# Cross-attention block on one core: scores of two heads in two neighbouring PSUM banks, one ScalarE eviction for both, with order and places laid out anew

## The chip, the cores and the metric

The kernel runs on one core of a Trainium2 chip. The metric is the device time of one execution in microseconds (us). The engines are TensorE (PE, with its weight loads PEld), VectorE (DVE), ScalarE (ACT), GpSimd (POOL) and SyncE (SP), which issues the DMA transfers. Each engine takes its instructions strictly in order.

## The reference

All data are fp32. x and the context are 8 batches of 256 tokens by 512. There are 16 heads of 32, and the inner width of the last part is 2048.

```python
h = layer_norm(x, ln1_w, ln1_b)
q, k, v = (h @ q_w + q_b, ctx @ k_w + k_b, ctx @ v_w + v_b)   # 16 heads of 32
scores = where(mask, q @ k.T / sqrt(32), lowest)
out = softmax(scores) @ v
hidden = out @ cproj_w + cproj_b + x
y = gelu(layer_norm(hidden, ln2_w, ln2_b) @ fc_w + fc_b)      # 512 -> 2048
result = hidden + y @ proj_w + proj_b                          # 2048 -> 512
```

## The kernel before, in words

The tokens are worked in two halves, g = 0 and 1, of four batches (1024 tokens). The projections of q, k, v and the output `o` are done as 2 x 2 blocks with seven products instead of eight (P1 to P7, `quad`, L848); their sums of operands run on DVE and POOL (`sums`, names ending in t1 to t4, s1 to s4), and their results are added up from three PSUM banks X, Y and W (names such as k0_0_c11). The fc and proj layers use the same scheme on two levels (`grown2`), with weight sums that are stored to DRAM (fcd, prd) and loaded again (fl, pl).

Attention works in 32 units: g, a group hg of four heads, and a batch b; the names carry the three digits, so unit 020 is half 0, heads 8 to 11, batch 0. `scores` (L1009) lets PE compute, for each of the four heads j and each half kc of the keys, a block of 128 keys by 256 queries (operation s020). The four heads use 32 rows of PE each and run side by side; each head has a PSUM bank of its own. ACT then evicts each of the eight blocks (ev020_30 is head 3, key half 0) and adds a bias for each key, the mask, from `cols`. The result lies in two buffers pr of two heads each. DVE takes the maximum over the keys (mx, mt, fold; ACT moves three small pieces, mc), SP stores the maxima (md) and loads them as a broadcast to all partitions (mm). POOL or DVE subtracts them (less), ACT takes the exponential of two heads at a time (exp), and `attend` (L1057) lets PE compute the sums and the products with v in 32-column tiles (av). DVE inverts the sums (r) and scales (att). So there is a long chain between s and av of a unit, and PE works on other things meanwhile.

PE's instructions are of three kinds: full 128 x 128 matmuls, the 32-row tiles of s and the 32-column tiles of av. A transposition (turn, `turned`, L710) is a full matmul of 128 columns into a PSUM bank, four to a bank; its eviction (y0_10, L775) applies the layer norm's weight and bias. The second layer norm of half 0 has eight such groups, turn_y0_00 to turn_y0_31, and the first fc products are fc001_P1 and fc011_P1.

The order is written out: `PROGRAM` is a list of all operations by name, with a letter where an engine has to be chosen (V, A, G for DVE, ACT, POOL). `Order.run` (L94) goes through it and emits each operation's instructions on its engine. `PLACES` (L355) gives each buffer its slot in SBUF or PSUM; a later user of a slot waits for the earlier one. PSUM has eight banks of 512 columns. Three (tags W0 to W2) hold X, Y and W of the products, five (C0 to C4) the scores, av and the transpositions, unless `PLACES` names a tag of the other set.

Of the kernel before, what the change touches and what calls it, by code (L numbers as in the profile page):

```python
# [10 lines left out]
F32 = mybir.dt.float32  # L11
# [5 lines left out]
P = 128  # L17
# [6 lines left out]
BANKS = {"W": 3, "C": 5}  # L24
# [19 lines left out]
class Order:  # L44
# [49 lines left out]
    def run(self):  # L94
# [30 lines left out]
cq0_00_1 cq0_00_0 vw00 cq0_01_1 cq0_01_0 rows8 rows7 cq0_10_0 turn_c0_00 rows0 turn_c0_10 c0_00:A cq0_10_1 c0_10:V  # L125
cq0_11_0 small v0_0_P1 cq0_11_1 kw01 turn_c0_11 fw0_01_0 v0_1_P1 c0_11:A vw11 rows5 turn_c0_01 rows2 turn_c0_30
vw10 c0_01:A turn_c0_20 mk c0_30:A c0t1:G c0_20:V v0_0_t1:A vw01 turn_c0_21 v0_1_t1:V turn_c0_31 fw0_11_1 k0_0_P2
c0_21:V rows3 c0_31:V c0t2:V kw10 k0_1_P2 rows4 kw11 c0t3:V kw00 rows6 v0_0_P2 vws1:V fw0_10_0 c0t4:V fw0_00_0
v0_1_P2 vws2:V fw0_00_1 kws1:V xt0_3 rows1 k0_1_P1 fw0_10_1 kws2:V mk~1 xt0_0 kws3:V fw0_11_0 v0_0_c11 fw0i1_1:G
v0_1_P6 fw1_00_1 vws4:V xt0_2 fw0i1_2:V fw0s3:V fw1_00_0 k0_0_P1 v0_1_t2:A xt0_6 fw0i7_1:V fw1_10_0 v0_1_c11  # L130
fw0i7_2:G fw1_11_0 cols v0_1_P5 cols~1 qw10 k0_0_t1:V qw11 fw0i7_4:V fw0s1:V xt0_1 v0_0_P6 v0_1_t3:A fw1_11_1
fw0s2:V fw1_10_1 xt0_5 k0_0_P6 fw0i6_3:V xt0_4 k0_1_t1:V fw0i6_1:G cb fw0i5_1:G v0_1_P3 k0_0_t2:V kws4:G fw0i1_4:V
k0_1_P6 stats_x0_30 fw0i1_3:G fw1i1_1:V stats_x0_00 fw0i6_2:G k0_0_P5 fw1i1_3:V k0_1_t2:A xt0_7 v0_0_t2:V fw1i1_2:G
fw0_01_1 stats_x0_10 fw1i1_4:G fcd0_1_True aggr_x0_30 k0_1_P5 fw1i4_1:V qw01 aggr_x0_00 stats_x0_01 fw1i4_2:G
fw1_01_0 fw0i6_4:V fcd0_6_False stats_x0_11 k0_1_P7 k0_1_t3:A fw1_01_1 aggr_x0_01 fw0i7_3:V k0_0_t3:A eps_x0_0
fcd0_7_False stats_x0_31 pow_x0_0 qw00 aggr_x0_31 k0_1_P3 fw1i4_4:G k0_1_c22 fcd0_7_True fw0i5_2:G aggr_x0_11
# [12 lines left out]
fw0i4_3:G fcd1_5_True mc000_3 mc000_2 s020 cb1_13 mc000_1 fw1i6_3:G fold000 cb1_00 fw1i7_1:V q0_0_P3 md000 ev020_30
fw0i4_1:V ev020_21 fw1i7_2:V cb1_23 ev020_00 fw0i4_2:G cb1_21 ev020_10 fw1i7_4:G ev020_20 cb1_01 q0_1_P7 ev020_01  # L150
cb1_11 fw1i3_1:G ev020_31 q0_0_c12:A mx020_1 fw1i6_2:G ev020_11 s002 fw1i3_2:G mm000 mx020_0 fw0i4_4:G v0_1_P7
fw1i7_3:G mt020 stats_x1_11 mc020_2 mc020_3 fw1i6_4:G q0_1_t3:V ev002_30 ev002_11 fw1i3_4:G aggr_x1_10 aggr_x1_11
v0_0_P7 mc020_1 q0_1_c22 ev002_01 ev002_00 fold020 ev002_10 eps_x1_1 md020 ev002_31 pow_x1_1 ev002_20 q0_1_P3
fcd1_7_True v0_0_c22 ev002_21 cb1_31 nb_x1_1 mx002_0 less000_1:G mm020 s022 mx002_1 cb1_33 cb1_22 v0_0_P4 ev022_20
cT1_10 cb1_32 ev022_30 cT1_00 ev022_11 cb1_30 less000_0:G ev022_31 mt002 v0_1_c22 ev022_21 q0_1_P4 ev022_00 mx022_1
mc002_2 ev022_01 ev022_10 less020_0:G mx022_0 v0_1_P4 mt022 q0_1_c21 mc022_2 mc022_3 s010 mc022_1 v0_0_c21 mc002_3
exp000_0 less020_1:G cT1_01 k1_0_P1 fold022 mc002_1 ev010_20 q0_1_c12:V md022 exp000_1 v0_1_c21 fcd1_6_True cT1_20
fcd1_3_True k1_1_P1 ev010_10 ev010_31 fold002 ev010_11 cT1_11 md002 cT1_30 av000 vd0_0_11 k1_0_t1:A cT1_21 mm022
c1t1:G ev010_21 kd0_0_12 ev010_01 cT1_31 ev010_30 kd0_1_12 exp020_0 k1_0_P2 r000 mm002 ev010_00 exp020_1 att000
c1t2:V s030 norm_x1_11:A c1t3:V av020 xd1_3 ev030_10 norm_x1_10:A fcd0_4_True less022_1:G mx010_1 ev030_11 xd1_2  # L160
k1_1_t1:A k1_0_P6 xt1_7 mx010_0 ev030_21 ku003 ev030_01 ev030_20 kd0_0_22 k1_0_c11 ev030_30 ev030_31 k1_1_P6 mt010
# [12 lines left out]
mx001_0 s021 xd1_1 v1_1_t1:A ku031 norm_x1_00:A mt001 k1_1_c21 ku011 av030 ev021_00 xd1_0 norm_x1_21:V v1_0_t1:A
less032_1:G ev021_10 norm_x1_20:A v1_1_P6 mc001_3 less032_0:V xd1_4 ev021_31 ev021_20 xd1_5 mc001_2 mc001_1
vd0_1_11 ev021_30 v1_0_P6 fold001 ev021_11 ev021_21 md001 less012_0:G ev021_01 mx021_1 ku023 exp032_0 ku013 v1_0_P2
r030 exp032_1 xb1_21 xb1_20 v1_1_t2:A att030 s003 less012_1:V v1_0_t2:A mm001 av032 xb1_01 mx021_0 ev003_20
ev003_11 xb1_22 ev003_21 xb1_23 ev003_10 mt021 ev003_00 v1_0_P5 ev003_31 r032 exp012_0 att032 ev003_30 mc021_1
v1_1_P5 mx003_1 mc021_2 ev003_01 less001_0:G mc021_3 exp012_1 fold021 s023 v1_0_c11 md021 v1_1_t3:A mx003_0 xb1_13
av012 xb1_10 ev023_00 less001_1:G ev023_01 mt003 v1_0_t3:V ev023_31 ev023_21 mc003_2 v1_0_P7 mc003_3 r012 ev023_20  # L180
ev023_30 mc003_1 ev023_10 att012 ev023_11 xT1_20 s011 exp001_0 fold003 mx023_0 md003 v1_1_P2 ev011_00 mm021
ev011_31 xb1_12 ev011_11 ev011_20 xb1_11 exp001_1 v1_1_P3 xb1_03 v1_1_c11 ev011_30 mx023_1 ev011_01 ev011_21
# [329 lines left out]
def tile_xattn_block(  # L512
# [41 lines left out]
    halves = {}  # L554

    def tile_of(b):
        if b.t is None:
# [941 lines left out]
```

## Time and profile before

| | us |
|---|---|
| three runs: median (lowest, highest) | 662.69 (662.54, 663.8) |
| span of the profiled execution | 662.0 |
| PE busy in it | 654.6 |
| DVE busy | 585.7 |
| ACT busy | 342.4 |
| POOL busy | 374.8 |

Times in the profile are microseconds from the span's start unless marked ns. A group of instructions reads: line, engine, operation, what it writes and reads, partitions x elements, count; then busy time in total, mean ns of one, and the idle time of the engine ahead of them with what ended it. A row of a timeline starts with start and duration of a run of like instructions; idle time ahead of it, with what ended it, stands in brackets. The ends of matmuls are modelled, so a busy PE isn't PE at its peak. A wait is put down to the semaphore that came last.

### The profile page before, as it was taken

To read this page: it belongs to the slowest core of one execution; us is meant where nothing else is said; L and a number is where in the kernel's file an instruction comes from. 1 tells how busy PE (TensorE), PEld (TensorE's weight loads), DVE (VectorE), ACT (ScalarE), POOL (GpSimd) and SP (SyncE) were. 2 spreads that over 40 slices of the span, in tenths; PEclk is the share of its full clock that TensorE was granted. 3 is DMA by queue.
4 is the path that set the end of the run, shared out by engine and by line. 5 is a ranking of instruction groups with operands and counts; after the bars stand their busy time and mean duration, and the time that the engine had idled before them with its cause. 6 is when DMAs were issued, how large, how long until landed. Compare 5 with 4: busy or idle time off the path is not lost.

```text
span 662.0 us, 11469 instructions
## 1 busy us (share of the span) xinstructions
PE 654.6 (99%) x3925; PEld 490.0 (74%) x3925; DVE 585.7 (88%) x980; ACT 342.4 (52%) x702; POOL 374.8 (57%) x340
## 2 busy tenths in 40 slices
PE   8999999999999999999999999999999999999997
PEld 7746554477544776777688888888888888888887
DVE  2998799999999999999999998997789787998775
ACT  2046479799999899866995572030020013930000
POOL 1262773646888997699958774423535217720260
PEclk9999999999999999999999999999999999999999
DMA  8999888786574467886878698889978779359366
GB/s 250 311 356 307 211 197 291 267 255 125 144 241 161 144 202 234 263 268 197 266 249 273 198 235 225 289 269 230 195 193 241 190 201 242 93 142 240 106 141 111
DMA packets 206586, 144.84 MB, mean 219 GB/s; under 512 B 117008, under 2 KB 166976, under 8 KB 206528
## 3 DMA queue, kind: packets, MB, share of 16 engines
q1 hardware_dynamic: 206528, 144.11, 76.8%
q8 instruction: 31, 0.51, 0.3%
q14 instruction: 27, 0.22, 0.1%
HBM read 104.10 MB, written 39.98 MB: 218 GB/s over the span
## 4 chain that ended last, share of the span: by engine, by line
PE 92%; DVE 5%; ACT 1%; DMA 1%; issue 0%; SPq 0%; POOL 0%; DVEq 0%; ACTq 0%
PE pd_X L639 15%; PE fc_X L639 14%; PE fc_W L639 8%; PE av L639 7%; PE pd_W L639 7%; PE s L639 4%; PE o_X L639 4%; PE q_X L639 4%; PE k_X L639 4%; PE v_X L639 4%; PE pd_Y L639 4%; PE fc_Y L639 4%; PE q_W L639 2%; PE k_W L639 2%; PE v_W L639 2%; PE o_W L639 2%
## 5 line engine op out<-in xcount | busy, mean ns | idle before, releaser
L1047 POOL TENSOR_TENSOR pr<-pr,mm 128x512 f32<-128x512 f32 x84 | 110.4, 1346 | 22.8 <-DMA mm<-md 9.2
L619 ACT ACTIVATE pr<-s,cols 128x256 f32<-128x256 f32 x256 | 104.5, 482 | 21.8 <-PE s L639 15.8
L1022 DVE TRANSPOSE_TENSOR_REDUCE mx<-pr 128x32 f32<-128x1024 f32 x64 | 77.6, 1223 | 3.3 <-ACT pr L619 3.3
L1227 ACT ACTIVATE h<-h,cols 128x256 f32<-128x256 f32 x128 | 54.1, 498 | 36.7 <-DVE h L630 36.6
L1050 ACT ACTIVATE pr<-pr 128x1024 f32<-128x1024 f32 x64 | 66.9, 1069 | 3.4 <-POOL pr L1047 2.8
L630 DVE TENSOR_TENSOR h<-fc_X,h 128x512 f32<-128x512 f32 x80 | 52.8, 679 | 6.2 <-PE fc_X L639 5.5
L630 DVE TENSOR_TENSOR h<-fc_W,h 128x512 f32<-128x512 f32 x48 | 32.0, 679 | 5.8 <-PE fc_W L639 5.3
L639 PE MATMUL av<-pr,ones 128*32 128x256 f32 x512 | 34.2, 384 | 0.7 <-ACT pr L1050 0.6
L1029 ACT COPY mx<-mx 32x64 f32<-32x64 f32 x96 | 23.1, 243 | 19.8 <-DVE mx L1026 15.8
L1042 DVE TENSOR_TENSOR pr<-pr,mm 128x1024 f32<-128x1024 f32 x22 | 30.8, 1407 | 0.0
L628 POOL TENSOR_TENSOR z1i<-h,z1i 128x512 f32<-128x512 f32 x4 | 5.7, 1440 | 40.4 <-PE pd_X L639 40.4
L639 PEld LDWEIGHTS av<-pr,ones 128*32 128x32 f32 x512 | 14.1, 109 | 18.5 <-issue 6.7
L630 POOL TENSOR_TENSOR h<-h,fl 128x512 f32<-128x512 f32 x9 | 11.5, 1295 | 24.6 <-DVE fl L630 15.0
L639 PE MATMUL fc_W<-y1i,fl 128*128 128x256 f32 x100 | 24.6, 380 | 0.0
L639 PE MATMUL fc_X<-y1i,fl 128*128 128x256 f32 x88 | 21.6, 381 | 0.0
L639 PEld LDWEIGHTS fc_W<-y1i,fl 128*128 128x128 f32 x100 | 18.9, 190 | 2.9 <-DVE h L630 0.3
L639 PE MATMUL pd_W<-z0i,pl 128*128 128x256 f32 x88 | 20.6, 379 | 0.0
L1030 DVE TENSOR_REDUCE mx<-mx 32x32 f32<-32x256 f32 x32 | 18.4, 574 | 1.4 <-ACT mx L1029 1.3
L639 PE MATMUL pd_X<-z0i,pl 128*128 128x256 f32 x80 | 18.9, 379 | 0.0
L606 ACT COPY fl<-fc_X 128x512 f32<-128x512 f32 x6 | 3.5, 580 | 29.5 <-PE fc_X L639 29.2
L639 PEld LDWEIGHTS fc_X<-y1i,fl 128*128 128x128 f32 x88 | 16.6, 190 | 2.6 <-ACT h L606 0.2
L639 PEld LDWEIGHTS pd_W<-z0i,pl 128*128 128x128 f32 x88 | 16.7, 190 | 2.3
(595 smaller groups left out, 1815.6 us busy)
## 6 DMA issues: line engine op xcount, KB each, us to landing
mm<-md SPq DMA_DIRECT2D x32, 512.0 KB, 5.1
pl<-prd SPq DMA_DIRECT2D x47, 256.0 KB, 4.2
fl<-fcd SPq DMA_DIRECT2D x41, 256.0 KB, 4.0
fl<-prd SPq DMA_DIRECT2D x24, 256.0 KB, 3.8
fw<-in_L_xattn_fc_w_dram SPq DMA_DIRECT2D x16, 256.0 KB, 4.9
pw<-in_L_xattn_proj_w_dram SPq DMA_DIRECT2D x32, 128.0 KB, 3.6
hid<-in_x_dram SPq DMA_DIRECT2D x8, 512.0 KB, 4.8
hd<-hid SPq DMA_DIRECT2D x8, 512.0 KB, 3.4
```

What stands on the lines that cost most here:

```text
L606: (nc.scalar.copy if e == "ACT" else nc.vector.tensor_copy)(to(), of_())
L619: lambda e: nc.scalar.activation(to(), of_(), AF.Identity, bias=bias(), scale=1.0))
L628: nc.gpsimd.tensor_tensor(to()[:, ts(k, 512)], in0()[:, ts(k, 512)], in1()[:, ts(k, 512)], op)
L630: E[e].tensor_tensor(to(), in0(), in1(), op)
L639: nc.tensor.matmul(o(), l(), r(), start=first, stop=True, skip_group_check=True)
L1022: T.op(f"mx{u}_{h}", [("DVE", 1.126)], [(pr[h], None)], [(mx, [h])], lambda e, h=h: nc.vector.tensor_reduce(tile_of(mx)[:, 0:64].rearrange ...
L1029: lambda e, a=a: nc.scalar.copy(tile_of(mx)[0:32, 64 + 64 * a : 128 + 64 * a], tile_of(mx)[32 * a : 32 * a + 32, 64:128]))
L1030: T.op(f"fold{u}", [("DVE", 0.38)], [(mx, [2, 3, 4, 5])], [(mx, [6])], lambda e: nc.vector.tensor_reduce(tile_of(mx)[0:32, 320:352], tile_ ...
L1042: nc.vector.tensor_tensor(p_, p_, m_[:, :, None, :].to_broadcast([P, 2, 2, S]), ALU.subtract)
L1047: E[e].tensor_tensor(p_, p_, at(M, j)[:, None, :].to_broadcast([P, 2, S]), ALU.subtract)
L1050: lambda e, h=h: nc.scalar.activation(tile_of(pr[h]), tile_of(pr[h]), AF.Exp), table="exp")
L1227: lambda e, f=f, b=b, c=c: nc.scalar.activation(at(h[f][b], c), at(h[f][b], c), AF.Gelu_apprx_tanh, bias=col(c_fcb + f * 4 + c), scale=1.0 ...
```

## The change

The scores of two heads now share one buffer s of 1024 columns in two neighbouring banks (kind D, tags B0 to B3, where banks 2s and 2s+1 form Bs). Each head still has a bank of its own. One ACT instruction evicts, for one half of the keys, 256 columns out of either bank: 512 elements. So a unit has four evictions instead of eight (ev020_10: pair 1, half 0). The buffer pr is laid out by key half first and head second; the maximum, the subtraction, the sum of halves and the operands of av are indexed accordingly. On POOL a subtraction is still two instructions of 512, on DVE one of 1024. There are no sets of banks any more: any buffer may lie in any of the eight, and a score buffer takes an even-numbered pair.

```diff
-BANKS = {"W": 3, "C": 5}
+BANKS = ("W", "C", "D")
...
-                    w = where[b.name]
-                    b.home = w[0] if not w[0].isdigit() else b.kind
-                    b.slot = int(w.lstrip("WC"))
+                    b.slot = int(where[b.name])
...
+            elif b.kind == "D":
+                b.t = banks.tile([P, 1024], F32, tag=f"B{b.slot // 2}", name=b.name)
+                twos[b.slot // 2] = None
             else:
-                b.t = banks.tile([P, 512], F32, tag=f"{b.home}{b.slot}", name=b.name)
+                s, k = divmod(b.slot, 2)
+                if twos.get(s) is None:
+                    twos[s] = banks.tile([P, 1024], F32, tag=f"B{s}", name=b.name)
+                b.t = twos[s][:, ts(k, 512)]
...
-        sb = [Buf(f"s{u}_{j}", "C", 2) for j in range(4)]
+        sb = [Buf(f"s{u}_{h}", "D", 4) for h in range(2)]
...
-            for j in range(4):
-                copy(f"ev{u}_{j}{kc}", (pr[j // 2], [2 * (j % 2) + kc]), (sb[j], [kc]), lambda j=j, kc=kc: at(pr[j // 2], 2 * (j % 2) + kc),
-                     lambda j=j, kc=kc: at(sb[j], kc), 256, lambda kc=kc: col(2 * (4 * g + b) + kc))
+            for h in range(2):
+                T.op(f"ev{u}_{h}{kc}", [("ACT", 0.62)], [(sb[h], [kc, 2 + kc]), (cols, None)], [(pr[h], [2 * kc, 2 * kc + 1])],
+                     lambda e, h=h, kc=kc: nc.scalar.activation(
+                         at(pr[h], kc, 1, 512).rearrange("p (i q) -> p i q", i=2),
+                         tile_of(sb[h]).rearrange("p (i k q) -> p i k q", i=2, k=2)[:, :, kc, :],
+                         AF.Identity, bias=col(2 * (4 * g + b) + kc), scale=1.0))
...
+                m_ = at(M, 2 * h, 2)
                 if e == "DVE":
-                    p_ = tile_of(pr[h]).rearrange("p (i k q) -> p i k q", i=2, k=2)
-                    m_ = tile_of(M)[:, 512 * h : 512 * h + 512].rearrange("p (i q) -> p i q", i=2)
-                    nc.vector.tensor_tensor(p_, p_, m_[:, :, None, :].to_broadcast([P, 2, 2, S]), ALU.subtract)
+                    p_ = tile_of(pr[h]).rearrange("p (k n) -> p k n", k=2)
+                    nc.vector.tensor_tensor(p_, p_, m_[:, None, :].to_broadcast([P, 2, 512]), ALU.subtract)
                     return
-                for i in range(2):
-                    j = 2 * h + i
-                    p_ = at(pr[h], i, 1, 512).rearrange("p (k q) -> p k q", k=2)
-                    E[e].tensor_tensor(p_, p_, at(M, j)[:, None, :].to_broadcast([P, 2, S]), ALU.subtract)
+                for k in range(2):
+                    p_ = at(pr[h], k, 1, 512)
+                    E[e].tensor_tensor(p_, p_, m_, ALU.subtract)
```

PROGRAM and PLACES are new throughout; PROGRAM has 2825 words instead of 2953, since four evictions a unit are gone. The piece around one operation, pow_y0_0, in each:

```diff
-pow_y0_0 stats_y0_11 aggr_y0_11 eps_y0_3 exp110_0
+exp110_1 eps_y0_0 less120_1:G pow_y0_0 aggr_y0_11 mm112 av122 less110_0:V ev101_00 hd1 pw0_10_00 av102 av130 ev101_11
```

Three places of the new order follow. First ACT, the evictions of unit 020 in the list before (s_0 to s_3 are the four heads' banks; pr_0 and pr_1 the two buffers they go to):

```order
L619 ACTIVATE pr_1_785<-s_3_769,cols 128x256
L619 ACTIVATE pr_1_785<-s_2_767,cols 128x256
L619 ACTIVATE pr_0_791<-s_0_763,cols 128x256
L619 ACTIVATE pr_0_791<-s_1_765,cols 128x256
L619 ACTIVATE pr_1_785<-s_2_767,cols 128x256
L619 ACTIVATE pr_0_791<-s_0_763,cols 128x256
L619 ACTIVATE pr_1_785<-s_3_769,cols 128x256
L611 ACTIVATE v_0_11_290<-q_0_X,cols 128x512
L619 ACTIVATE pr_0_791<-s_1_765,cols 128x256
```

And the same place on ACT in the new list, the evictions of unit 020 (s_0_734, s_1_737) and the first of unit 002, where s_0 and s_1 are pairs of banks:

```order
L1002 ACTIVATE pr_0_752<-s_0_734,cols 128x512
L1002 ACTIVATE pr_1_766<-s_1_737,cols 128x512 x2
L1002 ACTIVATE pr_0_752<-s_0_734,cols 128x512
L1002 ACTIVATE pr_1_801<-s_1_791,cols 128x512
L1002 ACTIVATE pr_0_803<-s_0_788,cols 128x512
```

Eight instructions of 256 elements became four of 512.

Second PE, at the first av. Before, after the last rows of s010, two k products (k1_0_P1 and k1_1_P1, in banks k_0_X and k_1_X) stand ahead of av000:

```order
L639 MATMUL s_2_938<-q_0_11_665,qw_404 128x256
L639 MATMUL s_3_940<-q_0_11_665,qw_404 128x256
L639 MATMUL k_0_X<-c_00_901,kw_325 128x512 x2
L639 MATMUL k_1_X<-c_00_901,kw_325 128x512 x2
L639 MATMUL av_980<-pr_0_693,ones 32x256 x2
L639 MATMUL av_980<-pr_1_695,ones 32x256 x2
```

In the new list av000 (av_901) follows s010 (s_0_880 and s_1_883) on PE directly; the first of the k products stands ahead of s010 (in the bank named first):

```order
L621 MATMUL first<-c_00_769,kw_238 128x512 x2
L621 MATMUL first<-vw_304,c0t_452 128x256 x4
L621 MATMUL s_0_880<-xn_x_21_539,k_0_11_384 128x256 x2
L621 MATMUL s_1_883<-xn_x_21_539,k_0_11_384 128x256 x2
L621 MATMUL s_0_880<-xn_x_21_539,k_0_11_384 128x256 x2
L621 MATMUL s_1_883<-xn_x_21_539,k_0_11_384 128x256 x2
L621 MATMUL av_901<-pr_0_678,ones 32x256 x2
L621 MATMUL av_901<-pr_1_697,ones 32x256 x2
```

So PE reaches av000 with fewer products done since s000.

Third PE, at the first transpositions of the second layer norm, half 0. Before, two groups (turn_y0_00 into ps_y_00, turn_y0_10 into ps_y_10) are followed by the first fc product and by an av:

```order
L726 MATMUL ps_y_00_2793<-ident,xn_y_01_2760 128x128
L726 MATMUL ps_y_10_2809<-ident,xt_1_1174 128x128
L726 MATMUL ps_y_10_2809<-ident,xn_y_01_2760 128x128
L726 MATMUL ps_y_10_2809<-ident,xn_y_10_2751 128x128
L726 MATMUL ps_y_10_2809<-ident,xn_y_01_2760 128x128
L639 MATMUL fc_X<-y_00_2805,v_0_11_290 128x256 x2
L639 MATMUL av_2836<-pr_0_2486,ones 32x256 x2
```

In the new list all four groups of the first token half stand ahead of the first fc products (names in PSUM are those of a pair's first user: turn_y0_00 and turn_y0_20 are in ps_y_00, turn_y0_10 and turn_y0_30 in av_2252, and fc011_P1 goes to av_2521). The last eight rows of it on PE:

```order
L709 MATMUL av_2252<-ident,vw_217 128x128
L709 MATMUL av_2252<-ident,xn_y_01_2519 128x128
L709 MATMUL av_2252<-ident,k_0_11_384 128x128
L709 MATMUL av_2252<-ident,xn_y_01_2519 128x128
L709 MATMUL av_2252<-ident,vw_217 128x128
L709 MATMUL av_2252<-ident,xn_y_01_2519 128x128
L621 MATMUL av_2521<-y_00_2611,q_0_12_729 128x256 x2
L621 MATMUL ps_y_00_2573<-y_00_2611,fl_0_2502 128x256 x2
L621 MATMUL ps_y_00_2573<-pr_0_2233,ones 32x256 x2
```

ACT evicts turn_y0_20 ahead of turn_y0_00 there, and the first fc product reads y0_00.

More of the change, by code (lines that the diff above doesn't have):

```diff
@@ L157 @@
[L157 to L161, printed above, removed]
@@ new lines @@
+kd0_1_12 q0_1_P1 v0_1_c12:A kd0_0_22 turn_x0_21 vd0_0_11 x0_21:A x0t1:V fw1s2:V q0_0_P2 x0t2:V fcd0_2_True cb1_22
+q0_1_P2 q0_1_t1:V q0_0_P6 q0_0_c11 x0t3:V q0_0_t2:V q0_1_P6 fw1i1_3:V kd0_1_11 cb1_03 s000 q0_0_P5 fcd0_6_True
+kd0_0_11 ev000_01 fw1s4:G qws3:G q0_1_t2:V q0_0_P7 x0t4:G cb1_01 xt1_4 stats_x1_20 stats_x1_10 kd0_0_21 ev000_10 vu010
+fw0i4_1:V fw0i4_2:G kd0_0_12 qws4:G cb1_11 cb1_13 q0_1_P5 q0_0_t3:V q0_0_c22 q0_0_P4 ev000_00 ev000_11 mx000_1
+fw0i4_4:V q0_0_P3 fw0i4_3:V mx000_0 mt000 cb1_23 mc000_3 fw1i3_1:G cb1_21 q0_0_c12:A fw1i3_2:G q0_0_c21 cb1_12 s020
@@ new lines @@
+mx002_0 ev022_11 fw1i7_1:G k1_0_P1 ev022_01 md020 v0_1_c22 cb1_31 q0_1_c21 v0_1_P4 mx002_1 pow_x1_1 mx022_1
+fcd1_3_True v0_0_c21 less000_1:G ev022_00 s010 exp000_1 mt002 cT1_11 fw1i7_2:V nb_x1_1 cT1_01 mx022_0 less000_0:G
+exp000_0 av000 mm020 cb1_32 fcd1_5_True mt022 ev010_01 cb1_33 k1_1_P1 v0_1_c21 fw1i7_3:G mc022_1 mc022_2 mc022_3
+fold022 cT1_30 fw1i7_4:G less020_1:G ku033 fcd1_7_True cT1_31 mc002_1 ku031 r000 c1t1:V att000 mc002_3 cT1_21 k1_0_P2
+exp020_1 ev010_10 md022 vd0_0_21 less020_0:G c1t3:G ev010_00 ev010_11 mc002_2 xt1_5 exp020_0 c1t2:V k1_1_t1:A s030
@@ new lines @@
+norm_y0_11:A av120 pw0_11_11 r102 less112_0:G pw0_11_01 pw0_10_11 hd3 r110 norm_y0_10:A turn_y0_00 att102 eps_y0_3
+nb_y0_2 exp112_1 att110 turn_y0_20 mx101_0 turn_y0_10 turn_y0_30 r122 y0_20:A pw0_10_10 pow_y0_3 less132_0:G pw0_11_10
+y0_00:A fl012_0 norm_y0_20:A exp112_0 fc011_P1 fl001_2 r120 fl016_2 y0_10:A norm_y0_21:A att130 nb_y0_3 norm_y0_30:A
+fc011_t1:A fc001_P1 less132_1:V av112 att120 att122 exp132_1 exp132_0 fc001_P2 y0i1_1:G pw0s3:V hd0 y0i1_2:G
+fc001_t1:A fc011_P2 fl001_3 mx101_1 fc011_c11 pw0i7_1:G norm_y0_31:A mt101 fl016_3 fc001_c11 y0_30:A fc011_P6 r112
@@ L552, in tile_xattn_block @@
     E = {"PE": nc.tensor, "DVE": nc.vector, "ACT": nc.scalar, "POOL": nc.gpsimd, "SP": nc.sync}
-    halves = {}
+    halves, twos = {}, {}
     def tile_of(b):
@@ L646, in tile_xattn_block @@
     nc.vector.memset(warm, 1.0)
-    first = banks.tile([P, 512], F32, tag="W0", name="first")
+    twos[0] = banks.tile([P, 1024], F32, tag="B0", name="first")
+    first = twos[0]
     def small(n):
```

645 lines of the change are left out of this document (306 added, 339 removed).

## The prediction

> **What bounds the kernel now.** I read the page first: the busy times, then the chain that ended last.
>
> ```profile
> span 662.0 us, 11469 instructions
> PE 654.6 (99%) x3925; PEld 490.0 (74%) x3925; DVE 585.7 (88%) x980; ACT 342.4 (52%) x702; POOL 374.8 (57%) x340
> PE 92%; DVE 5%; ACT 1%; DMA 1%; issue 0%; SPq 0%; POOL 0%; DVEq 0%; ACTq 0%
> ```
>
> TensorE (PE) is busy 654.6 of 662.0 us and makes 92% of the chain. Whatever else the change saves, it counts only where PE stands still or where PE itself works longer than it must. ScalarE (ACT), whose evictions are changed, is half idle. Second, the busy time by stage (columns: PE, PE weight load, DVE, ACT, POOL with instructions, then PE clock, DMA share, GB/s), to see where PE stands:
>
> ```profile
> 0.00:8.00 8.00, 6.28 (x46) 5.66 (x47) 0.80 (x2) 1.87 (x2) 0.80 (x8) 1.00 0.70 220
> ...
> 60.00:115.00 55.00, 55.00 (x323) 27.98 (x325) 49.59 (x76) 39.51 (x90) 32.02 (x31) 1.00 0.86 234
> 115.00:200.00 85.00, 84.88 (x677) 49.97 (x670) 80.56 (x139) 79.33 (x168) 57.20 (x41) 1.00 0.73 206
> 200.00:260.00 60.00, 58.95 (x548) 39.52 (x550) 58.75 (x112) 54.15 (x115) 54.54 (x45) 1.00 0.59 182
> 260.00:330.00 70.00, 68.89 (x554) 50.24 (x547) 67.35 (x117) 53.12 (x107) 61.11 (x62) 1.00 0.77 247
> ...
> 658.00:662.00 4.00, 0.64 (x6) 0.45 (x5) 0.42 (x1) 0.00 (x0) 0.00 (x0) 0.95 0.38 119
> ```
>
> PE's 7.4 idle us lie in three places: 1.72 at the start (loads), 3.36 at the end (last eviction and store), and 0.12 + 1.05 + 1.11 = 2.28 between 115 and 330, the attention stages and the second layer norm. The ends are built alike in both kernels, so only the 2.28 can be won as idle time. The clock is 1.00 in all working stages, so no throttle is to be won or lost. ACT, half idle on the whole, is 93% busy from 115 to 200 and 90% from 200 to 260: there the evictions do crowd it. DVE is 95%, 98% and 96% busy in the three stages. Third, what PE waits for by name (total, times, longest):
>
> ```profile
> PE ps_y L726 <- DVE att L630: 1.2, 2, 1.0
> ...
> PE av L639 <- ACT pr L1050: 0.6, 1, 0.6
> PE v_X L639 <- DMA vw<-in_L_xattn_v_w_dram: 0.5, 1, 0.5
> PE fc_Y L639 <- DVE h L630: 0.2, 1, 0.2
> ```
>
> No wait for a score eviction is among them. The named ones from 115 on are 2.0 us.
>
> **The change part by part.** First the matmuls. The two lists hold the same 2015 of them, so their own time stays. What differs is how often PE goes from full 128x128 matmuls to the scores' 32-row tiles (s), to the 32-column tiles of probabilities times values (av), and back. Starts of the PE timeline price such a stretch:
>
> ```profile
> 74.14 1.15 PE L639 MATMUL s<-q,v 32*128 32x256 f32 x16
> 75.21 1.98 PE L639 MATMUL q_X<-x,q 128*128 128x512 f32 x4
> 77.03 1.88 PE L639 MATMUL q_W<-x0t,kws 128*128 128x512 f32 x4
> 78.84 1.15 PE L639 MATMUL s<-v,k 32*128 32x256 f32 x16
> ...
> 259.57 1.07 PE L639 MATMUL av<-pr,ones 128*32 128x256 f32 x16
> 260.46 1.05 PE L639 MATMUL av<-pr,vws 128*32 128x256 f32 x16
> 261.44 1.13 PE L639 MATMUL fc_X<-y,q 128*128 128x256 f32 x4
> ...
> 263.28 1.03 PE L639 MATMUL fc_X<-y0i,kws 128*128 128x256 f32 x4
> 264.14 1.03 PE L639 MATMUL fc_X<-y0i,fl 128*128 128x256 f32 x4
> ```
>
> Inside one mode four matmuls of 256 columns take 264.14 - 263.28 = 0.86 us, 0.216 each, 0.43 for 512 columns; sixteen s or av matmuls, four side by side, ought to take 0.865. The s group took 75.21 - 74.14 = 1.07, so 0.21 over; the full stretch behind it 78.84 - 75.21 = 3.63 for eight of 0.43 (3.44), 0.19 over; the av stretch 261.44 - 259.57 = 1.87 for 1.73, 0.14 over. Counted in the two lists, the s stretches stay 32, the av stretches go from 26 to 22 and the full ones from 41 to 39: 4 x 0.14 + 2 x 0.20 = **0.96 us less**, on the path itself. Bounds: 0.5 (if only one side of a transition costs) to 1.3 (all six at 0.21).
>
> Second the evictions. The rows: the old eviction; a 512-wide one with the same bias from one bank; the same from SBUF.
>
> ```profile
> L619 ACT ACTIVATE pr<-s,cols 128x256 f32<-128x256 f32 x256 | 104.5, 482 | 21.8 <-PE s L639 15.8
> ...
> L619 ACT ACTIVATE att<-att,cols 128x512 f32<-128x512 f32 x16 | 11.4, 724 | 0.4 <-DVE att L630 0.3
> ...
> L611 ACT ACTIVATE q<-q_X,cols 128x512 f32<-128x512 f32 x5 | 3.3, 686 | 1.8 <-issue 1.5 <-PE q_X L639 0.3
> ```
>
> A unit (four heads of one batch) pays 8 x 104.5/256 = 3.27 us now, and 4 x 0.67 (3.3/5) to 4 x 0.71 (11.4/16) after: 2.7 to 2.85. So 0.4 to 0.55 is saved, 13 to 18 us over 32 units. That the two halves lie in two banks has no row; if the instruction paid for two single ones (2 x 0.482 = 0.96) a unit would cost 3.86, 0.6 more. I take 0.5 saved, since the same engine, bias and element count have rows and the strided reads of the old form show nothing odd. None of it lies on PE's path by itself: it only moves everything behind it in a unit's chain (column maximum on DVE, its store md and broadcast load mm, subtraction, exp, av) 0.5 earlier.
>
> The Trainium skill, "ScalarE: Activation LUTs", What ACT_TABLE_LOAD costs, gives 280 ns + 0.833 ns an element for an instruction with such a bias, overlapping its neighbour by 93 ns: my estimate from it is 8 x 0.40 against 4 x 0.61, 0.75 saved. The measured 512-wide rows say less (0.67); by the page the next term would be 0.1 us smaller.
>
> Third, cover in the first units. In the new list av000 stands right behind s010, where two k products stood between; and av020 follows s020 sooner.
>
> ```profile
> 60.84 1.15 PE L639 MATMUL s<-q,xt 32*128 32x256 f32 x16
> ...
> 96.44 1.07 PE L639 MATMUL av<-pr,ones 128*32 128x256 f32 x16
> ...
> 101.29 1.07 PE L639 MATMUL av<-pr,ones 128*32 128x256 f32 x16
> ```
>
> ```profile
> 90.88 4.97 POOL L1047 TENSOR_TENSOR pr<-pr,mm 128x512 f32<-128x512 f32 x4 [0.83 <-DMA mm<-md]
> ```
>
> ```profile
> 94.34 1.05 ACT L1050 ACTIVATE pr<-pr 128x1024 f32<-128x1024 f32 x1
> ...
> 99.50 1.08 ACT L1050 ACTIVATE pr<-pr 128x1024 f32<-128x1024 f32 x1
> ```
>
> From s000 to av000 the list before has 26 matmul rows of 512 columns, 16 of 256, five s groups, in five s and five full stretches: 26 x 0.86 + 16 x 0.432 + 5 x 0.865 + 5 x 0.41 = 35.6, and the trace has 96.44 - 60.84 = 35.6 (a row of the list is two matmuls of the trace). The new list has 18 of 512 and four full stretches: 28.5. For s020 to av020 it is 27.15 before (101.29 - 74.14) and, with two 512 rows and a stretch fewer, 25.25 after. Unit 020's last exp ended at 100.58, so its chain took 26.45. With evictions 0.5 shorter 25.9 is left, 0.65 too long; but between the end of its subtractions (95.85) and the start of its last exp lie 3.65 us, of which only one other exp (1.07) is its own: 2.5 us is ACT queue, which gets lighter. So 0 to 0.65, and I take 0.2. Unit 000 ended its last exp at 95.39, 34.55 after s000: if every queue stood as before, it would be 34.55 - 0.5 - 28.5 = 5.5 late. But unit 020's chain shows that 16.74 from s to the start of subtraction is enough; with 4.97 and two exps that is 23.9. I take nothing; the 5.5 is a rival's price.
>
> Fourth, the second layer norm's transposes. The row where PE waits now, the eviction behind such a group, and the later wait for an exp:
>
> ```profile
> 258.12 0.33 PE L726 MATMUL ps_y<-ident,xt 128*128 128x128 f32 x1 [1.00 <-DVE att L630]
> ...
> 283.96 1.07 PE L639 MATMUL av<-pr,ones 128*32 128x256 f32 x16 [0.62 <-ACT pr L1050]
> ```
>
> ```profile
> L775 ACT ACTIVATE y<-ps_y,cols 128x512 f32<-128x512 f32 x8 | 6.0, 777 | 0.1
> ```
>
> The 1.00 is a wait for a bank (att120 on DVE still reads it). With the new places the banks of the first three groups have been free for long, and the fourth hangs on att102, further back. What is late next: all four groups now come ahead of the first fc product, which reads y0_00, and ACT evicts y0_20 first. From the end of the second group two evictions take 2 x 0.777 = 1.55, while two groups of four (4 x 0.109 each) cover 0.87: about 0.7 to 0.8 of wait. Net **-0.2**, ends -1.0 (evictions in time) and +0.9 (another eviction late). The 0.62 of av132 waits for an exp with three units' evictions ahead of it on ACT, 1.5 us lighter now: -0.3, ends -0.62 and 0.
>
> The subtractions' new layout has one more broadcast dimension or one fewer, same width; the masked maximum and av only index otherwise: no time. SP issues the same 598 transfers.
>
> **Sum.** 662.0 - 0.96 - 0.2 - 0.3 + 0.2 = 660.7 us of span. The profiled 662.0 stands 0.69 below the median of the runs, 662.69, so **661.4 us**. A measurement tells 0.2% from nothing, 1.3 us: faster means under 661.4, slower over 664.0; the forecast sits on the first edge.
>
> **The rivals.**
>
> *Late first units (slower).* The new list leaves av000 only 28.5 us of PE work. For: the old chain took 34.55, and DMA, which carries md and mm, is at 0.86 share there. Against: the 23.9 that unit 020 needed. It decides once the chain of unit 000 is over 28.5. Half of the 5.5 and 020's 0.65 make 3.4: 662.0 - 0.96 + 3.4 + 0.69 = 665.1. Chance 0.17.
>
> *The idle goes (more gained).* ACT is lighter by 13 to 18 us where it was full, four banks can serve any buffer, and most later units have a longer way from s to av in the new list. All 2.28 gone: 662.0 - 0.96 - 2.28 + 0.69 = 659.5; matmul ends are modelled, so short refills hide in PE's busy time, and I leave 1.5 for these: 658.0. For: the named waits are of banks and exps, which the change touches. Against: the new fc wait. Chance 0.28.
>
> *Two banks cost two reads.* +0.6 a unit, on an ACT that has 5.7 us free from 115 to 200, where some 15 units would add 9: 3.3 come through, 662.0 - 0.96 + 3.3 + 0.69 = 665.0. Chance 0.04.
>
> *POOL against DVE.* By the lists POOL has 24 more 512-wide instructions, DVE 12 fewer 1024-wide.
>
> ```profile
> L1047 POOL TENSOR_TENSOR pr<-pr,mm 128x512 f32<-128x512 f32 x84 | 110.4, 1346 | 22.8 <-DMA mm<-md 9.2
> ...
> L630 DVE TENSOR_TENSOR x1t<-x,x x1: 2110/2110/2110, 175.8 to 175.8; 128x1024 f32<-128x1024 f32 x1
> ...
> L630 DVE TENSOR_TENSOR a0t<-att,a0t x1: 1200/1200/1200, 225.2 to 225.2; 128x1024 f32<-128x1024 f32 x1
> ```
>
> The same DVE addition of two SBUF operands took 2.11 us in one place and 1.20 in another. If POOL's work beside it is the reason, 24 x 1.35 = 32 us more of POOL take up to 32 x 0.91/2.11 = 14 from DVE, and its 12 instructions give back at least 14: nothing on the whole. If a third of the loss falls from 200 to 260, where DVE has 1.25 free, 4.6 - 1.25 = 3.4 reach PE: 665.1. The Trainium skill, "SBUF — State Buffer", Who interferes with whom, states that a VectorE instruction with two SBUF inputs contends with a GpSimd instruction that reads SBUF, which speaks against the change; no row of this trace isolates it. Chance 0.05.
>
> *Nothing measurable.* The transitions' 0.96 is eaten by new waits of the same size: 661.5 to 663.9. Chance 0.12, beside the forecast's own 0.34.
>
> **Numbers.** The forecast's own range is 660.4 to 662.5; about half of it lies under 661.4. Faster: 0.17 + 0.28 = 0.45; within 0.2%: 0.17 + 0.12 = 0.29; slower: 0.17 + 0.04 + 0.05 = 0.26. The range goes from the idle's end, 658.0, to the slower rivals' 665.2, leaving out their upper halves.
>
> **What would show it.** Right: 512-wide evictions of 0.67 to 0.71 by total over count; PE's busy time about 1 us less; no ps_y wait for att, but a 0.7 wait of the first fc product for y; av000 without a wait. Late units show as av waiting for exp near 90 to 100 us. Two reads show as 0.96 an eviction. POOL against DVE shows as over 98% of DVE with PE waiting for its products. A sum of new waits above 2.5 us, or a PE busy time not lower, proves me wrong.

## The result, and the profile after

The changed kernel takes 798.4 us (median of four runs, 793.9 to 806.1), the kernel before 663.25 us beside it: 1.2006 times as long, 95% interval 1.1955 to 1.2058. The forecast was 661.4 us. Ratios, here and in the table below, leave out disturbed runs (here the one of 806.1 us), while medians count all runs.

The page of the changed kernel, the lines that answer to those of before:

```profile
span 792.1 us, 11334 instructions
...
PE 691.2 (87%) x3925; PEld 500.1 (63%) x3925; DVE 574.9 (73%) x968; ACT 323.3 (41%) x571; POOL 402.1 (51%) x366
...
PEclk9999999998998999899899998999999999999999
...
PE 22%; DVE 4%; POOL 2%; issue 2%; DMA 1%; SPq 1%; ACT 0%; POOLq 0%
```

No engine is full any more: DVE fell from 88% to 73%, PE from 99% to 87%. PE idles 792.1 - 691.2 = 100.9 us where it idled 7.4, and its busy time grew by 36.6. These make up the 130.1. The clock row no longer holds 9 throughout; the mean granted clock was 0.967, which is worth at most 26 us (3.3% of the span). The rest of the longer busy time has no row of its own; a group of matmuls that starts after a wait is drawn a little longer (1.98 us at 35.05 below, where its like take 1.88), and such restarts are many. The chain's shares add up to some 32% only, so I take nothing from that line.

Where it is lost, by stage (the same columns as before):

```profile
14.00:60.00 46.00, 43.50 (x159) 26.45 (x157) 41.25 (x84) 18.85 (x29) 15.76 (x18) 1.00 0.92 309
60.00:115.00 55.00, 47.98 (x260) 24.80 (x260) 41.28 (x65) 24.52 (x46) 31.92 (x30) 1.00 0.83 241
115.00:200.00 85.00, 71.89 (x557) 43.32 (x550) 60.05 (x110) 56.80 (x97) 49.33 (x42) 0.96 0.62 163
200.00:260.00 60.00, 52.06 (x345) 24.44 (x345) 43.51 (x74) 41.38 (x71) 35.47 (x29) 0.89 0.34 108
...
560.00:650.00 90.00, 79.47 (x356) 66.22 (x356) 58.21 (x110) 12.86 (x22) 41.47 (x42) 1.00 0.78 178
650.00:720.00 70.00, 62.47 (x271) 51.34 (x272) 51.24 (x69) 24.62 (x58) 29.77 (x23) 0.98 0.64 151
```

In the kernel before, PE did not stand still at all in the stages that answer to the first and to the last of these:

```profile
14.00:60.00 46.00, 46.00 (x164) 28.11 (x164) 43.15 (x85) 15.73 (x23) 21.00 (x25) 1.00 0.99 336
...
560.00:658.00 98.00, 98.00 (x465) 86.23 (x464) 81.94 (x124) 22.23 (x55) 34.12 (x26) 1.00 0.59 139
```

It is lost everywhere: before there are any scores (14 to 60 us) and in the fc and proj stages long after the last one (560 to 720). By operation: s000 starts 10.6 us later than before, s100 35.9, the first fc product of half 0 49.6, the last av 84.4, and the transposition that was last before (turn_o01) 125.9. A part of the first figure is the new order (in e1 below, where every bank is a tile of its own, s000 starts 4.4 us late). A cause in the scores alone can't do that. What does PE wait for?

```profile
PE ps_y L621 <- DVE h L612: 10.7, 10, 2.3
PE av L621 <- DVE hid L612: 7.1, 3, 5.0
PE ps_y L621 <- ACT h L588: 5.1, 2, 3.1
PE av L621 <- DVE h L612: 3.9, 3, 2.6
PE first L621 <- DVE qws L612: 3.6, 1, 3.6
```

It waits for evictions of products (h, hid, qws). The names in front (ps_y, av, first) are those of a pair of banks by its first user. One such wait in the first stage, on PE, and then what DVE and ACT did there:

```profile
27.95 3.65 PE L621 MATMUL v_X<-c0t,vw 128*128 128x512 f32 x8
31.44 1.88 PE L621 MATMUL v_X<-c0t,xt 128*128 128x512 f32 x4
35.05 1.98 PE L621 MATMUL ps_c<-c0t,kws 128*128 128x512 f32 x4 [1.74 <-DVE qw L612]
36.87 1.88 PE L621 MATMUL first<-c,kw 128*128 128x512 f32 x4
38.59 1.89 PE L621 MATMUL v_X<-vws,c0t 128*128 128x256 f32 x8
```

```profile
28.65 0.68 DVE L612 TENSOR_TENSOR k<-ps_c,k 128x512 f32<-128x512 f32 x1
...
34.34 0.65 DVE L612 TENSOR_TENSOR qw<-ps_c,qw 128x512 f32<-128x512 f32 x1
```

```profile
40.52 0.69 ACT L593 ACTIVATE xt<-v_X,cols 128x512 f32<-128x512 f32 x1 [2.01 <-PE v_X L621]
```

At 35.05 PE writes k0_1_P7 into bank 6. The last reader of bank 6 was DVE's addition at 28.65, done at 29.33. PE waits all the same until the addition at 34.34 ends at 34.99: that one reads v0_1_Y, in bank **7**, the other half of the tile B3. The ACT row shows the other direction: k0_1_t2 reads bank 3, whose matmuls (k0_1_P6, the second half of the row at 27.95) were done at 31.60, and it is let go when a product into bank 2 of the same tile (v0_1_P5, at 38.59) is done, at 40.48. I did this, by matching the trace with PROGRAM and PLACES, for every PE operation that starts over 0.15 us later than its forerunner's matmuls allow: its start against the ends of its inputs, of its own bank's users, and of evictions from the bank next door. Of 107 such gaps, 118.5 us in all, the eviction next door ended last in 54, with 79.8 us; inputs or the own bank in 30, with 32.4. DVE and ACT, too, sat idle ahead of evictions that began as a matmul into the bank next door ended, with their own bank done before: DVE for some 60 to 90 us and ACT for some 10 to 20, depending on how long before. So the theory: **two banks that are halves of one tile wait for each other**. PLACES gives a bank for each buffer, but the program's waits are kept for each tile, and the change made eight tiles into four.

### The profile page after: what moved, and what is told of

Read it like the earlier page. It is cut to its first block, busy times and chain, and to the rows that moved or that the text cites. A ratio compares the mean times of both kernels' runs of the same rounds, so it can differ in the third digit from the quotient of the medians.

```text
span 792.1 us, 11334 instructions
## 1 busy us (share of the span) xinstructions
PE 691.2 (87%) x3925; PEld 500.1 (63%) x3925; DVE 574.9 (73%) x968; ACT 323.3 (41%) x571; POOL 402.1 (51%) x366
## 5 line engine op out<-in xcount | busy, mean ns | idle before, releaser
L1002 ACT ACTIVATE pr<-s,cols 128x512 f32<-128x512 f32 x128 | 80.8, 686 | 52.2 <-PE s L621 36.0
L612 DVE TENSOR_TENSOR h<-ps_y,h 128x512 f32<-128x512 f32 x45 | 30.5, 680 | 18.9 <-PE ps_y L621 17.4
L1015 ACT COPY mx<-mx 32x64 f32<-32x64 f32 x96 | 23.1, 243 | 48.9 <-DVE mx L1012 35.6
L612 DVE TENSOR_TENSOR h<-av,h 128x512 f32<-128x512 f32 x43 | 29.0, 680 | 18.4 <-PE av L621 17.8
L790 POOL TENSOR_TENSOR rs_y<-rs_y,neg_half 128x2 f32<-128x2 f32 x8 | 10.4, 1307 | 21.7 <-DVE rs_y L787 19.9
L610 POOL TENSOR_TENSOR z1i<-z1t,z1i 128x512 f32<-128x512 f32 x8 | 10.9, 1390 | 20.2 <-DVE z1i L612 20.2
L612 DVE TENSOR_TENSOR h<-fc_X,h 128x512 f32<-128x512 f32 x23 | 15.7, 684 | 7.4 <-PE fc_X L621 7.0
L621 PE MATMUL av<-pr,ones 128*32 128x256 f32 x272 | 18.9, 397 | 1.5 <-ACT q L593 0.9
L610 POOL TENSOR_TENSOR z0i<-z0t,z0i 128x512 f32<-128x512 f32 x8 | 11.0, 1391 | 16.4 <-DVE z0t L612 8.3
L621 PE MATMUL av<-h,pl 128*128 128x256 f32 x40 | 11.3, 434 | 5.0 <-DVE hid L612 5.0
L1061 DVE STREAM_TRANSPOSE r<-rc 128x256 f32<-128x256 f32 x32 | 14.3, 445 | 1.1
```

The costliest lines, as they stand in the source:

```text
L610: nc.gpsimd.tensor_tensor(to()[:, ts(k, 512)], in0()[:, ts(k, 512)], in1()[:, ts(k, 512)], op)
L612: E[e].tensor_tensor(to(), in0(), in1(), op)
L621: nc.tensor.matmul(o(), l(), r(), start=first, stop=True, skip_group_check=True)
L1002: lambda e, h=h, kc=kc: nc.scalar.activation(at(pr[h], kc, 1, 512).rearrange("p (i q) -> p i q", i=2), tile_of(sb[h]).rearrange("p (i k q) ...
L1015: lambda e, a=a: nc.scalar.copy(tile_of(mx)[0:32, 64 + 64 * a : 128 + 64 * a], tile_of(mx)[32 * a : 32 * a + 32, 64:128]))
L1061: nc.vector.transpose(tile_of(R).rearrange("p (n r) -> p n r", r=32), tile_of(rc)[:, 8:16, None].to_broadcast([P, 8, 32]))
```

## The experiments

Theory A is this. Theory B: the new order. Theory C: the instruction that reads two banks. Ratios are against the kernel before on the same chip.

| run | median us | before | ratio, 95% interval |
|---|---|---|---|
| e1 changed order, eight tiles, split evictions | 673.0 | 665.2 | 1.0109 (1.0066 to 1.0151) |
| e2 before, four shared tiles | 736.3 | 665.2 | 1.1069 (1.0971 to 1.1168) |
| e3 as e1, wide evictions of one bank | 671.8 | 665.2 | 1.0075 (1.0033 to 1.0116) |
| e4 before, wide evictions of one bank | 664.9 | 665.2 | 1.0000 (0.9967 to 1.0033) |
| e5 as e1, two POOL sums moved | 678.8 | 663.5 | 1.0206 (1.0154 to 1.0259) |
| e6 as e3, masked in exp, sums moved | 672.1 | 663.5 | 1.0116 (1.0059 to 1.0172) |
| e7 before, one shared tile | 688.9 | 663.5 | 1.0371 (1.0310 to 1.0431) |
| e8 changed kernel, split evictions | 797.4 | 663.5 | 1.1983 (1.1919 to 1.2048) |
| e9 as e1, less111_0 on POOL | 669.9 | 665.7 | 1.0050 (1.0011 to 1.0089) |
| e10 as e6, less111_0 on POOL | 666.7 | 665.7 | 1.0010 (0.9969 to 1.0052) |
| e11 as e1, two sums on DVE | 668.5 | 665.7 | 1.0044 (1.0004 to 1.0085) |
| e12 before, other pairs | 735.6 | 663.8 | 1.1084 (1.1052 to 1.1115) |

**Which of the three.** e1 takes the shared tiles out of the changed kernel:

```diff
             elif b.kind == "D":
-                b.t = banks.tile([P, 1024], F32, tag=f"B{b.slot // 2}", name=b.name)
+                b.t = [banks.tile([P, 512], F32, tag=f"B{b.slot + i}", name=f"{b.name}{i}") for i in range(2)]
             else:
...
+                b.t = banks.tile([P, 512], F32, tag=f"B{b.slot}", name=b.name)
...
+                         at(pr[h], 2 * kc + i), tile_of(sb[h])[i][:, ts(kc, 256)],
+                         AF.Identity, bias=col(2 * (4 * g + b) + kc), scale=1.0) for i in range(2)])
```

> The changed kernel's order and places, but every PSUM bank is a tile of its own (eight of 512 columns) and each two-bank eviction is two of 256 columns. Theory A (two banks that share one 1024-column tile make PE wait for evictions of the neighbouring bank): the waits that the new trace shows go, 658 to 672 us, near before. Theory B (the new order itself is bad: late chains, fewer products as cover): it stays near 790 us, 780 to 800. Theory C (the two-bank eviction is what hurts): 660 to 680 as well, but then the next run stays at 663.

e2 puts them into the kernel before, and nothing else:

```diff
-                b.t = banks.tile([P, 512], F32, tag=f"{b.home}{b.slot}", name=b.name)
+                s, k = divmod(b.slot + (3 if b.home == "C" else 0), 2)
+                if s not in twos:
+                    twos[s] = banks.tile([P, 1024], F32, tag=f"B{s}", name=b.name)
+                b.t = twos[s][:, ts(k, 512)]
```

> The kernel before, order, places and evictions untouched; only its eight banks are now halves of four tiles of 1024 columns (W0 and W1, W2 and C0, C1 and C2, C3 and C4). Theory A: PE waits for evictions out of the neighbouring bank all over the program, 730 to 830 us. Theories B and C: 663 us, within 0.5%.

e8 keeps the changed kernel's tiles and splits the evictions (in the changed eviction, `for i in range(2)` over `at(pr[h], 2 * kc + i)` and `at(sb[h], 2 * i + kc)`):

> The changed kernel with its four shared tiles, but each two-bank eviction done as two of 256 columns, one bank each. Theory A: the shared tiles do it all, 790 to 810 us as the changed kernel. Theory C (one instruction that reads two banks is part of it): 3% or more under it, 775 or less.

e1 came to 673.0, e8 to 797.4, e2 to 736.3. With the same order, eight tiles bring 125 us back; with the same tiles, the narrow evictions bring nothing; and four tiles alone cost an untouched order 71 us. A holds, C falls, and of B some 1% is left. What PE waits for in e2, where the kernel before had no wait for a score eviction and one of 0.2 us for an h:

```profile
PE ps_c L642 <- ACT pr L622: 9.5, 10, 1.6
PE v_X L642 <- ACT pr L622: 5.8, 7, 1.5
PE ps_c L642 <- DVE h L633: 4.6, 8, 0.9
```

By the same matching as above, the eviction next door ended last in 48 of e2's 81 gaps of PE, with 42.1 of 64.4 us. One thing more differs in e2: each tile is kept for the whole program, where the kernel before takes a new tile for each buffer. What that alone costs, with eight tiles, was not tried.

**How much a shared tile costs.** e7 gives the kernel before one shared tile, for W0 and W1 (`if b.home == "W" and b.slot < 2`); e12 pairs each W bank with a C bank (`s, k = (b.slot, int(b.home == "C")) if b.slot < 3 else (3, b.slot - 3)`).

> The kernel before, with only W0 and W1, two of the three banks of the products, as halves of one tile; six single tiles. Theory A (a wait for each eviction next door): part of the second run's 73 us, since each product's two banks are then each other's neighbours: 675 to 715 us, waits all over the program. If a bank that shares costs only where scores are in the pair: 663.

> The kernel before once more on four shared tiles, with other neighbours: W0 with C0, W1 with C1, W2 with C2, C3 with C4. The second run (W0 W1, W2 C0, C1 C2, C3 C4) lost 71 us, W0 with W1 alone 25. If the loss depends on whose eviction stands next door, this pairing, where each product's bank has a bank of scores or av beside it and the product's own banks are apart, comes out at another figure: 700 to 790 us, over the second run's in the attention stages (to 400 us), and near 0 in the fc and proj stages if the C banks carry nothing there. If the number of shared tiles alone decides: 736 again, within 1%.

One tile costs 25 us (687.0 of span), with waits in the early stages and in the late ones:

```profile
73.03 1.98 PE L643 MATMUL first<-x0t,qw 128*128 128x512 f32 x4 [0.86 <-DVE q L634]
...
251.96 3.72 PE L643 MATMUL first<-vws,a0t 128*128 128x256 f32 x16 [1.16 <-DVE hid L634]
...
518.78 1.13 PE L643 MATMUL first<-y1i,pl 128*128 128x256 f32 x4 [0.79 <-DVE h L634]
```

The other pairing cost the same as the first, 735.6 against 736.3. My guess that the pairing would show was wrong, and by stage they agree too (s100 is 24.7 us late against 27.3, the last av 53.2 against 55.4). In the changed kernel, where any buffer may lie in any bank and the order was written for that, it is 1.8 times as much; which of the two makes the difference wasn't tried.

**What a wide eviction is worth.** e3 and e4 evict 512 columns out of one bank, both key halves of a head; both add the first half's mask values to the second half. In e4, whose list keeps four of a unit's eight eviction words, the edit is:

```diff
-                copy(f"ev{u}_{j}{kc}", (pr[j // 2], [2 * (j % 2) + kc]), (sb[j], [kc]), lambda j=j, kc=kc: at(pr[j // 2], 2 * (j % 2) + kc),
-                     lambda j=j, kc=kc: at(sb[j], kc), 256, lambda kc=kc: col(2 * (4 * g + b) + kc))
+            copy(f"ev{u}_{j}0", (pr[j // 2], [2 * (j % 2), 2 * (j % 2) + 1]), (sb[j], None), lambda j=j: at(pr[j // 2], j % 2, 1, 512),
+                 lambda j=j: at(sb[j], 0, 1, 512), 512, lambda: col(2 * (4 * g + b)))
```

> As the first run (changed order, eight tiles), but a unit's four evictions are 512 wide, each out of one bank: both key halves of one head. It leaves out that the second key half has mask values of its own (it adds the first half's). Beside the first run it tells what a wide eviction is worth by itself: ACT some 13 to 18 us less busy. Theory A, and ACT off PE's path: within 0.5% of the first run, 658 to 672 us. If the evictions' length were the point: 3 us or more under the first run. Theory B: near 790 us.

> The kernel before, but with a unit's eight evictions of 256 columns merged into four of 512, one for each head's bank at the place of its later one (it adds the first key half's mask values to both halves). If the shorter evictions were worth what the idle-goes rival took, up to 2.3 us less: 660.5 us. If ACT's time lies beside PE's and nothing waits for it: 662 to 664, no change.

e4 is at 1.0000. Its evictions, and those of the changed kernel, which read two banks:

```profile
L605 ACT ACTIVATE pr<-s,cols 128x512 f32<-128x512 f32 x128 | 81.3, 685 | 24.6 <-PE s L625 16.2
```

```profile
L1002 ACT ACTIVATE pr<-s,cols 128x512 f32<-128x512 f32 x128 | 80.8, 686 | 52.2 <-PE s L621 36.0
```

104.5 us became 81.3, and the time didn't move: ACT's time lies beside PE's. Two banks cost the same as one. In e4 PE waits 1.6 us for evictions, which now stand at the place of the later one, so a gain of that size could hide there; e3 against e1 (671.8 and 673.0), with the evictions in the same four places, is within their intervals too.

**What is left of the new order.** In e1 PE's largest wait is one of 4.7 us for an exp, and behind it stands a DVE instruction. PE, then DVE, then POOL of e1:

```profile
330.18 1.08 PE L617 MATMUL av<-pr,ones 128*32 128x256 f32 x8 [4.73 <-ACT pr L1029]
```

```profile
322.51 6.53 DVE L1022 TENSOR_TENSOR pr<-pr,mm 128x1024 f32<-128x1024 f32 x1
```

```profile
322.32 2.51 POOL L606 TENSOR_TENSOR y0t<-y,y0t 128x512 f32<-128x512 f32 x2
324.79 2.48 POOL L606 TENSOR_TENSOR y0t<-y,y 128x512 f32<-128x512 f32 x2
327.24 0.71 POOL L608 TENSOR_TENSOR y0i<-y0t 128x256 f32<-128x256 f32 x1
328.03 1.59 POOL L608 TENSOR_TENSOR y0i<-y0t,y0i 128x256 f32<-128x256 f32 x1
```

less111_0 took 6.53 us, where its like take 1.2 to 2.3, while POOL ran five instructions on end: the fifth ended at 327.95, and less111_0 1.09 us later. Its data were there: POOL subtracts the other half of the same unit, from the same mm, in the row before these. e5 moves the words y0t4:G and y0t3:G behind av111; e6 adds to that wide evictions without bias, exponentials of 512 with the mask as bias, and y0_00:A ahead of y0_20:A.

> The first run again (changed order, eight tiles, 256-column evictions, 670.9 us of span), with one thing moved: the POOL sums y0t4 and y0t3 stand behind av111 in the list instead of ahead of less111_0. Theory: the 4.7 us wait of av111 is DVE's less111_0 held up for 6.5 us while five POOL instructions run one after another; the wait goes, and with it the half clock behind it (some 1.7 us): span 664 to 666, and less111_0 at 1.2 to 2.3 us. Rival: the wait is a late chain (md, mm) and comes back as a wait for mm or exp: 669 to 672.

> All that pays so far, computing the whole block: changed order, eight tiles, four 512-wide evictions a unit from one bank each without bias, the mask added in the exponentials (four of 512 instead of two of 1024), the two POOL sums behind av111, and y0_00 evicted ahead of y0_20. If the sum of the parts holds (0.96 us of transitions, the 5 us wait and its half clock, the 0.7 us wait of the first fc product): 659 to 661.5 us of span, a ratio of 0.995 to 0.999. If ACT's longer exponentials come late: 663 to 667.

Neither did what I meant: a word further back in the list holds nothing up, POOL ran ahead of av111 as before, and the wait stayed (4.7 and 4.5). A second one had come, for a DVE instruction on two elements. DVE and POOL of e5:

```profile
116.75 0.18 DVE L778 BATCH_NORM_AGGREGATE mv_x<-st_x 128x2 f32<-128x6 f32 x1
116.96 6.99 DVE L782 TENSOR_SCALAR rs_x<-mv_x 128x2 f32<-128x2 f32 x1
123.87 0.68 DVE L776 BATCH_NORM_STATS2 st_x<-kw 128x6 f32<-128x512 f32 x1
```

```profile
116.50 2.51 POOL L606 TENSOR_TENSOR c1t<-c,c1t 128x512 f32<-128x512 f32 x2
118.98 4.94 POOL L1026 TENSOR_TENSOR pr<-pr,mm 128x512 f32<-128x512 f32 x4
```

It ends with POOL's sixth instruction (123.92). In e1 the same instruction, beside the same six of POOL, took 0.83 us. So e9 takes the DVE instruction away (`less111_0:G` right behind `less111_1:G`), e11 takes POOL's away (`y0t4:V y0t3:V` behind exp111_0), and e10 is e6 with less111_0 on POOL.

> Moving the two POOL sums in the list did nothing, since POOL ran ahead of av111 all the same: this run takes the disputed DVE instruction away instead. As the first run (changed order, eight tiles), with less111_0 on POOL behind less111_1. Theory (DVE held up behind a run of POOL instructions): the 4.7 us wait of av111 falls to about 1 us (two POOL halves 2.5, exp 1.05 from 327 on), 665 to 668 us of span unless another DVE instruction is held up elsewhere (one of 7 us was, near 117 us, in two of the four runs with eight tiles): 670 to 674 then. Rival (a late md, mm): 3 us or more of wait stay.

> As the first run, but the two sums y0t4 and y0t3 run on DVE behind less111_0, so that POOL has a pause there; less111_0 stays on DVE. Theory: less111_0 takes 1.2 to 2.3 us instead of 6.5 and av111's wait falls under 0.5 us: 664 to 667 us of span, or 670 to 674 if the hold-up near 117 us comes. Rival (less111_0 long for a reason of its own, operands or layout): it stays at 6.5 us.

> The whole block with the wide one-bank evictions and the mask in the exponentials, and less111_0 on POOL: the best sum of parts. 659 to 662 us of span if no DVE instruction is held up (0.995 to 1.0), 666 to 670 if the one near 117 us is.

In e11 the same instruction, with POOL at rest:

```profile
321.62 1.22 DVE L1022 TENSOR_TENSOR pr<-pr,mm 128x1024 f32<-128x1024 f32 x1
```

1.22 instead of 6.53, and av111's wait is gone; in e9 it is 0.5. DMA is no reason for the 6.53: its busy share was 1.06 around this row of e11 (321.6 to 322.9) and 0.93 in e1 from 322.5 to 325. The spans of e9 and e11, 667.4 and 666.7, lie in what was expected, under e1's 670.9; the medians' intervals against before overlap with e1's, so the gain of 3 to 4 us is shown by the rows more than by the ratios. e10, the best, is at 1.0010 (0.9969 to 1.0052): no version here beats the kernel before.

## Why the prediction was wrong

**The step that failed** is the one that counted banks as free one by one: "the banks of the first three groups have been free for long", and, among the rivals, "four banks can serve any buffer" as a gain. I worked out every slot from PLACES as a bank. The diff showed `b.t = twos[s][:, ts(k, 512)]`, two buffers as slices of one tile, and I gave that line no price and no rival. It made the two halves wait for each other in all stages: e2 shows 71 us for it alone, e1 gets 125 back. My range ended at 665.2; no rival of mine came over that.

**The transitions**, -0.96: not told apart. With the new order and eight tiles PE's busy time is 652.0 (e10), 653.4 (e11), 654.8 (e1) and 655.9 (e9); with the transitions of before it is 654.6, and 653.6 in e4. A term of 1 us can't be seen in these.

**The evictions**, 0.4 to 0.55 a unit: more. 128 of them took 80.8 us, so 4 x 0.631 = 2.52 against 3.27, 0.74 saved. The rows that I used, of evictions that mostly stand alone, hardly overlap with a neighbour (mean 0.686 and total over count 0.66, or 0.724 and 0.71), where these do (0.686 and 0.631). My estimate from the Trainium skill's "ScalarE: Activation LUTs" (What ACT_TABLE_LOAD costs) was 0.61 for an eviction and 0.75 saved; here the Trainium skill was nearer than my rows. That the saving lies off PE's path was right, by e4. Two reads for two banks: wrong, 0.686 us against 0.685.

**The first units**, 0 to 0.65: right in e1. av020 waits 0.22, and av000 starts at 94.66 without a wait, 29.4 us after s000, where before it was 35.6. (The 28.5 in the prediction adds up to 28.4 by its own terms; nothing hangs on that.) The rival of late first units falls.

**The second layer norm**: right in e1. The bank's 1.00 is gone, so is av132's 0.62, and the new wait that was worked out at 0.7 to 0.8 is there:

```profile
PE fc_X L617 <- ACT y L753: 0.7, 1, 0.7
```

**POOL against DVE**: it has no part in the measured 798.4, since no DVE instruction of the changed kernel took over 2.3 us. With eight tiles the mechanism is in e1, e3, e5 and e6, and the size was off. I priced it as a slowing by 0.91 of 2.11 us; it is a standstill of 5 us or more, and it comes at one or two places instead of everywhere. For this order with eight tiles the chance of 0.05 was too low. The Trainium skill, "SBUF — State Buffer", Who interferes with whom, states that a VectorE instruction with two SBUF inputs contends with a GpSimd one that reads SBUF; less111_0 is of that form, and 6.53 against 1.22 agrees.

**The sum.** Without the shared tiles the forecast's order came to 673.0, 1.1% over before, where 661.4 was forecast. In the profiled execution of e1 the 4.7 us wait and the half clock behind it (below) make some 6 of the 8.9 us over before; but e9 and e11, without that wait, are still 0.4 to 0.5% over it. So by the medians the wait explains about half, and the other half of what this order costs stays open.

## What to carry to other kernels

When a diff puts two buffers into one tile, read it as a wait between them, whatever the banks or addresses say: look for who writes the one while the other is read, and price each wait at an eviction and the queue ahead of it (1.5 us on average in the 54 waits above). Before merging instructions of an engine, ask for whom it is late; here a fifth less eviction time was worth nothing, with PE at 99%. And a long run of POOL instructions beside a DVE instruction that someone waits for is a risk of several us: leave POOL a pause there or give it that work too.

## What was not expected of the hardware

A wait costs more than its length. In e3, av111 waited 5.03 us; the granted clock around it (columns as above, the clock third from the end):

```profile
320.00:322.00 2.00, 0.10 (x4) 0.00 (x0) 2.00 (x1) 0.00 (x0) 2.00 (x2) 1.00 0.88 288
322.00:324.00 2.00, 0.00 (x0) 0.00 (x0) 2.00 (x2) 0.00 (x0) 1.92 (x3) 0.65 0.97 289
324.00:326.00 2.00, 0.87 (x11) 0.42 (x15) 2.00 (x3) 1.98 (x3) 1.95 (x3) 0.50 1.01 280
326.00:328.00 2.00, 2.00 (x24) 0.97 (x20) 1.84 (x4) 0.23 (x1) 1.98 (x3) 0.50 0.27 77
328.00:330.00 2.00, 2.00 (x12) 1.14 (x5) 1.09 (x4) 1.10 (x2) 2.00 (x4) 0.65 0.00 0
330.00:332.00 2.00, 2.00 (x21) 1.29 (x19) 1.51 (x6) 1.96 (x3) 0.90 (x2) 1.00 0.00 0
```

It fell to 0.50 some 2.5 us into the wait and came back only after 4 us of work: of the work from 325.1 to 330 most ran at half speed, which costs some 2 us more (2.9 us at 0.50 and 2 at 0.65 lose 1.45 and 0.7). The trace's clock records show these stretches at 0.50 with a length of 3.41 us or twice that: one of 6.83 from 322.59 in e3, but one of 3.41 from 329.65 in e1, where av111 waited 4.73 us, so that only some 1.4 us were lost. Waits of nearly the same length thus cost differently; ten such stretches make up nearly all of the changed kernel's 26 us. In the kernel before no wait of PE between two of its matmuls was longer than 1.0 us, and its clock stayed at 1.00 up to the last 4 us.

A DVE instruction can be held up by POOL over several POOL instructions: less111_0 for five of them, 6.53 us, which e11 shows by taking two of the sums away. One with two elements and a single input (116.96 above) took 6.99 us in e5; that POOL held it is argued from the times alone, since no run took POOL away there. By the section Who interferes with whom of the Trainium skill's "SBUF — State Buffer" such an instruction contends only in its two-port modes; no run here shows in which it ran. In the kernel before the longest DVE instruction, an addition of two SBUF operands beside POOL, took 2.33 us (487.65 to 489.98): POOL's first instruction there ended at 488.90, 1.08 us earlier. Why one waits for one POOL instruction and another for five or six stays open.
